# A deformable convolution prepared per batch, with the next layer's weight mixing beside its gathers

## The chip, the core and the metric

The kernel runs on one core of a Trainium2 chip. The core has a matrix engine (PE, with its own weight loads, PEld), a vector engine (DVE), a scalar engine (ACT), a general engine (POOL) and a queue that mainly starts transfers (SP); each works through its own queue of instructions in order, and they meet through semaphores. The metric is device time in microseconds (us) of one execution. The lower it is the better.

## The reference

A network of four layers on an input of 2 x 64 x 64 x 128 (two images, here called batches, of 4096 tokens with 128 channels), in float32. Layer 0 is a selective scan in four directions, layer 2 a state-space scan joined with a long spectral convolution, layer 3 attention and a mixture of experts. Layer 1, which the change rebuilds, is a deformable convolution on the group-normalised result x of layer 0, added to that result:

```python
offsets = conv(x, offset_w, 'SAME') + offset_b      # 3x3, 128 -> 18 channels
dy, dx = offsets[..., 0], offsets[..., 1]           # per pixel and tap
py, px = row + ky + dy, column + kx + dx
y0, x0 = floor(py), floor(px);  wy, wx = py - y0, px - x0
val = gather(y0, x0) * (1-wy)*(1-wx) + gather(y0, x0+1) * (1-wy)*wx
    + gather(y0+1, x0) * wy*(1-wx)   + gather(y0+1, x0+1) * wy*wx
out = einsum('bhwkc,kcf->bhwf', val, kernel) + bias # 9 taps, 128 -> 128
```

`gather` returns 0 outside of the image. Of layer 2 only one part matters here: before its convolution runs, 16 filters' matrices (`M_phi_plus`, `M_phi_minus`, four 128 x 128 each) are scaled and summed into mixed weights that depend on inputs alone.

## The kernel before

The activations X lie in SBUF as 64 tiles of 128 tokens x 128 channels (`k.X`, opened in pool `x01`), batch 0 in tiles 0 to 31, batch 1 in 32 to 63. `tile_hybrid_kernel` (L1375) calls `zero_table`, `layer0`, `layer1`, the function `work` inside `mixing_weights`, `norm_tokens` and then `layer2`.

**Who sets the order.** Outside of a few hand-ordered stretches (`tc.manual_schedule()`, in the scans of layers 0 and 2) a scheduler places the instructions when the kernel is built: each engine's queue is fixed then. Program order is the priority, and a later instruction that is ready may fill a gap. Tile pools are stacked in memory. A pool that is opened where a closed pool lay waits until all users of that pool are done. `bufs` is the number of copies of a tile that are used in turn.

**Layer 1** (L459) has a preparation and a gather loop.

The preparation runs over b = 0, 1:
- `to_channels` (L90; PE transposes L95, copies L72 alternating between DVE and ACT) makes `xt`, 128 channels x 4096 tokens.
- `zero_frame` clears the border of the padded image `xp` (66 x 66), on POOL. `groupnorm` (L126) takes statistics (L132, L133), runs a short chain on DVE, PE and ACT (L136 to L87) and scales `xt` in place (L146).
- POOL copies `xt` into `xp` (L485). PE transposes `xt` back to tokens, and copies make `xk`; eight transfers (L499, on SP's queue) write it into `table`, a tensor in DRAM of 2 x 67 x 67 cells with 4 x 128 numbers each: a cell holds the four neighbours that one bilinear sample needs. The table's border was zeroed at the start of the kernel by `zero_table`.
- The offset convolution: 8 column groups x 9 taps, matmuls of 128 x 18 weights on 512 columns (L505), output on 18 partitions; copies to `ot`; 32 transposes back to tokens (L510), and the offset bias (L511) gives `off`.

After both batches, DVE works out for all 64 tiles at once (tiles of 576 columns) the integer cell and the fractions (L526 to L537), the cell number `idx` (L538, L539) and the four weights `wt` (L543).

The gather loop runs over t = 0 to 63. Nine indirect transfers from POOL (L553) fetch 128 cells of 512 numbers each into `G` (3 buffers). DVE multiplies by the weights into `V` (L560, 2 buffers). PE sums the four neighbours and transposes in one step (L572, 36 matmuls against the identity), ACT copies to `vt` (L573), nine matmuls apply the kernel (L576), one adds the bias from a row of ones (L577), and DVE adds the result to X (L578). PSUM, of eight banks, is given out as 6 for the preparation, then 6 for `pv1` and 2 for `po2`.

**Mixing weights.** `mixing_weights` (L601) opens its pools `f2c` and `f2w` below those of layer 1. `work` is called after `layer1`, but its instructions can fill gaps earlier. It loads (L665, L666 for the 16 filters f), sums on DVE (L654, L656), scales (L669), adds and subtracts (L671, L672) and stores to DRAM. **`norm_tokens`** (L583) takes statistics of every tile of X (L590, L591) in a small pool `l2n` of its own, and from them the scale and shift for layer 2.

Of the kernel before, what the change touches and what calls it, by code (L numbers as in the profile page):

```python
# [158 lines left out]
def layer0(k):  # L159
# [3 lines left out]
    with ExitStack() as es:  # L163
# [26 lines left out]
        Y = big.tile([P, 2, L], F32, name="Y")  # L190
        zs = dr.tile([2, P, B * L], F32, name="zs")

        for b in range(B):
            Xb = X[:, b * NTB : (b + 1) * NTB, :]
            with ExitStack() as e2:
# [23 lines left out]
                for h in range(2):  # L219
# [6 lines left out]
                    for q in range(8):  # L226
# [10 lines left out]
                        nc.scalar.activation(U[:, h, q * N : (q + 1) * N], pc, AF.Silu, bias=k.v("conv_b")[:, h : h + 1])  # L237

# [167 lines left out]
            with ExitStack() as e2:  # L406
                wk = e2.enter_context(tc.tile_pool(name=f"l0f{b}", bufs=2))
                ps = e2.enter_context(tc.tile_pool(name=f"l0fs{b}", bufs=6, space=PSUM))
                for q in range(8):
# [24 lines left out]
                    nc.vector.tensor_tensor(o, po.rearrange("p (a c) -> p a c", c=C), o, ALU.add)  # L434

# [3 lines left out]
def zero_table(k, pool, table):  # L439


    nc = k.nc
    z = pool.tile([P, 4 * 4 * C], F32, name="zero")
    nc.gpsimd.memset(z, 0.0)
    flat = table.rearrange("a c -> (a c)")
    cell = 4 * C
    for b in range(B):
        at = b * TS * TS * cell

        for y in (0, TS - 2):  # L450
            rows = flat[at + y * TS * cell : at + (y + 2) * TS * cell].rearrange("(p f) -> p f", p=P)
            nc.gpsimd.dma_start(out=rows, in_=z[:, : 2 * TS * cell // P])

        edge = flat[at + (TS + TS - 2) * cell :]
        dst = bass.AP(edge.tensor, edge.offset, [[TS * cell, TS - 3], [1, 4 * cell]])
        nc.gpsimd.dma_start(out=dst, in_=z[: TS - 3, :])


def layer1(k, table):  # L459
    tc, nc, ins, X = k.tc, k.nc, k.ins, k.X  # L460
    with ExitStack() as es:
        enter = es.enter_context
        cst = enter(tc.tile_pool(name="l1c", bufs=1))
        wt = cst.tile([P, NT * 9, 4], F32, name="wt")
        idx = cst.tile([P, NT * 9], I32, name="idx")
        w_k = cst.tile([P, 9, C], F32, name="w_k")
        nc.sync.dma_start(out=w_k, in_=ins["kern1"].rearrange("t c f -> c t f"))

        with ExitStack() as e2:
            pre = e2.enter_context(tc.tile_pool(name="l1p", bufs=1))  # L470
            ps = e2.enter_context(tc.tile_pool(name="l1ps", bufs=6, space=PSUM))
            gmat = pre.tile([P, P], F32, name="gmat1")
            nc.sync.dma_start(out=gmat, in_=ins["gmat"])
            w_o = pre.tile([P, 9, 18], F32, name="w_o")
            nc.sync.dma_start(out=w_o, in_=ins["offw1"].rearrange("t c f -> c t f"))
            base = pre.tile([P, 2, NT, 9], F32, name="base")
            nc.sync.dma_start(out=base, in_=ins["base"])
            off = pre.tile([P, NT, 18], F32, name="off")
            for b in range(B):
                xt = pre.tile([P, L], F32, name="xt1")  # L480
                to_channels(k, ps, xt, lambda i: X[:, b * NTB + i, :], NTB)
                xp = pre.tile([P, 66, 66], F32, name="xp1", bufs=2)
                zero_frame(nc, xp)
                groupnorm(k, pre, ps, gmat, xt, "gn1")
                nc.gpsimd.tensor_copy(xp[:, 1:65, 1:65], xt.rearrange("p (h w) -> p h w", w=WW))  # L485

                xk = pre.tile([P, NTB, C], F32, name="xk")
                for g in range(0, NTB, 4):
                    pt = ps.tile([P, N], F32, name="pt1", tag="ps")
                    for j in range(4):  # L490
                        nc.tensor.transpose(pt[:, j * P : (j + 1) * P], xt[:, (g + j) * P : (g + j + 1) * P], k.ident)
                    k.copy(xk[:, g : g + 4, :].rearrange("p a c -> p (a c)"), pt)
                cells = table[b * TS * TS : (b + 1) * TS * TS, :].rearrange("(y x) c -> y x c", x=TS)
                for j in range(4):
                    dy, dx = divmod(j, 2)
                    for yy in range(2):
                        y0 = 2 - dy + yy
                        dst = cells[y0 : y0 + 63 : 2, 2 - dx : 66 - dx, j * C : (j + 1) * C]
                        nc.sync.dma_start(out=dst.rearrange("t x c -> x t c"), in_=xk[64 * yy : 64 * yy + 64, :, :])  # L499
                ot = pre.tile([18, L], F32, name="ot1")  # L500
                for q in range(8):
                    po = ps.tile([P, N], F32, name="po1", tag="ps")
                    for t in range(9):
                        ky, kx = divmod(t, 3)
                        nc.tensor.matmul(po[:18, :], w_o[:, t, :], xp[:, 8 * q + ky : 8 * q + ky + 8, kx : kx + WW], start=t == 0, stop=t == 8)  # L505
                    k.copy(ot[:, q * N : (q + 1) * N], po[:18, :])
                for g in range(0, NTB, 16):
                    pt = ps.tile([P, N], F32, name="pt2", tag="ps")
                    for j in range(16):
                        nc.tensor.transpose(pt[:, j * 18 : (j + 1) * 18], ot[:, (g + j) * P : (g + j + 1) * P], k.ident[:18, :18])  # L510
                    nc.vector.tensor_tensor(  # L511
                        off[:, b * NTB + g : b * NTB + g + 16, :],
                        pt[:, : 16 * 18].rearrange("p (a o) -> p a o", o=18),
                        k.r("offset_b").unsqueeze(1).to_broadcast([P, 16, 18]),
# [1011 lines left out]
```

## Time and profile before

| what | us |
|---|---|
| three runs | 15930.12, 15930.33, 15936.03 (median 15930.33) |
| the profiled execution | 15934.86 |
| its span in the profile | 15933.1 |
| PE busy | 12090.7 (76%) |
| DVE busy | 13888.6 (87%) |
| ACT busy | 9835.1 (62%) |
| POOL busy | 13460.0 (84%) |
| layer 0 (from the span's start) | to 4493.2 |
| layer 1, preparation | 4493.2 to 4693.60 |
| layer 1, gathers, first to last start | 4693.60 to 5663.64 |
| layer 1, last add to X (L578) | 5686.36 |
| first POOL work of layer 2 (L1101) | 5725.74 |

The span is the time from the first to the last recorded instruction; the execution is 1.8 us longer. Busy shares are means over stages with different limits: POOL's 84% comes mostly from the multiplications of the two scans, in layers 0 and 2, and says nothing of layer 1. A stage has to be read by itself, by its chain of waits (which work ended last, and what released it), its groups of instructions and its timeline. The mean granted PE clock over the span is 0.905 of full speed. The program has 190559 instructions.

### The profile page before, as it was taken

How to read it: one execution, taken by the hardware profiler on the slowest of the kernel's cores; microseconds unless marked ns; L12 is line 12 of the kernel's file. 1: busy time of each engine (PE TensorE's matmuls, PEld its weight loads, DVE VectorE, ACT ScalarE, POOL GpSimd, SP SyncE). 2: the span in 40 equal slices, each digit the busy share in tenths (PEclk: the TensorE clock that was granted, in tenths of full speed). 3: DMA queues.
4: the chain of work that ended last, by engine and by line, in shares of the span. 5: the costliest groups of instructions: out<-in, count | busy, mean ns of one | idle time of the engine just before them, and what ended most of it. 6: DMA issues, size and time to landing. Idle time of an engine off the chain costs nothing.

```text
span 15933.1 us, 190559 instructions
## 1 busy us (share of the span) xinstructions
PE 12090.7 (76%) x69566; PEld 7172.8 (45%) x69566; DVE 13888.6 (87%) x12159; ACT 9835.1 (62%) x15911; POOL 13460.0 (84%) x5142
## 2 busy tenths in 40 slices
PE   7666656666668854557887779879778898888897
PEld 2222222222238831334554546546445555555565
DVE  7999968999853379999999999999999999999974
ACT  5666526565500047777777677777777777777752
POOL 6888828888728889999999999999999999999960
PEclk9999989999988866778988889989999999999998
DMA  2111111111145544455565556556666665665543
GB/s 78 72 69 69 67 43 69 69 72 67 64 129 160 162 139 151 166 169 190 191 191 181 184 180 199 197 184 205 191 195 196 191 203 197 191 203 195 189 162 129
DMA packets 1211034, 2373.41 MB, mean 149 GB/s; under 512 B 346728, under 2 KB 923368, under 8 KB 1043952
## 3 DMA queue, kind: packets, MB, share of 16 engines
q1 hardware_dynamic: 1162672, 2206.74, 42.2%
q0 software_dynamic: 46560, 153.18, 3.3%
q8 instruction: 549, 8.99, 0.2%
q14 instruction: 389, 3.19, 0.1%
q10 hardware_dynamic: 864, 1.32, 0.0%
HBM read 2018.49 MB, written 342.41 MB: 148 GB/s over the span
## 4 chain that ended last, share of the span: by engine, by line
POOL 42%; DVE 16%; PE 14%; issue 6%; DMA 3%; ACT 3%; SPq 0%; POOLq 0%; DVEq 0%; ACTq 0%
POOL S L1101 36%; DVE S L1157 9%; PE pef L985 5%; DVE S L374 5%; POOL G L553 4%; DMA row<-drow 2%; PE Z L1119 2%; PE acc L958 2%; PE yp L403 1%; DVE M L388 1%; PE pw L784 1%; PE po L505 1%; POOL S L363 1%; POOL S L1107 1%; ACT ze L1125 0%
## 5 line engine op out<-in xcount | busy, mean ns | idle before, releaser
L1157 DVE TENSOR_TENSOR_SCAN S<-dA,S 128x512 f32<-128x512 f32 x8192 | 9222.6, 1198 | 391.9 <-ACT dA L1155 209.7
L1101 POOL TENSOR_TENSOR S<-row,g 128x4096 f32<-128x4096 f32 x1024 | 9102.4, 8896 | 255.6 <-DMA row<-drow 217.2
L1155 ACT ACTIVATE dA<-row,a_t 128x512 f32<-128x512 f32 x8192 | 5617.1, 692 | 2150.0 <-DVE S L1157 2113.9
L1119 PE MATMUL Z<-S,cv 128*32 128x256 f32 x32768 | 2498.8, 435 | 1488.5 <-ACT ze L1125 1248.9
L985 PE MATMUL pef<-hk,ur 128*128 128x256 f32 x14336 | 3508.6, 388 | 140.4 <-ACT e L965 122.0
L985 PEld LDWEIGHTS pef<-hk,ur 128*128 128x128 f32 x14336 | 2642.3, 191 | 1080.1 <-issue 564.8
L374 DVE TENSOR_TENSOR_SCAN S<-dA,S 128x1024 f32<-128x1024 f32 x1024 | 2339.2, 2284 | 243.5 <-ACT dA L372 98.1
L363 POOL TENSOR_TENSOR S<-du,br 128x1024 f32<-128x1024 f32 x1024 | 2407.8, 2354 | 138.2 <-DVE M L388 82.3
L1119 PEld LDWEIGHTS Z<-S,cv 128*32 128x32 f32 x32768 | 1000.9, 121 | 2690.9 <-issue 1290.0
L403 PE MATMUL yp<-M,ident 128*128 128x512 f32 x4096 | 2067.7, 629 | 2.9 <-DVE M L388 2.9
L403 PEld LDWEIGHTS yp<-M,ident 128*128 128x128 f32 x4096 | 821.8, 201 | 2087.8 <-issue 2049.1
L372 ACT ACTIVATE dA<-dt,an 128x511 f32<-128x511 f32 x2048 | 1406.9, 687 | 208.1 <-DVE S L374 131.2
L388 DVE TENSOR_TENSOR M<-S,pcn 128x1024 f32<-128x1024 f32 x1024 | 1250.6, 1221 | 106.4 <-DVE S L374 3.2
L332 PE MATMUL pcn<-cs,sel 80*128 80x512 bf16 x1024 | 408.5, 399 | 1174.6 <-DVE M L388 1157.6
L1125 ACT COPY ze<-Z 128x512 f32<-128x512 f32 x1024 | 1123.1, 1097 | 223.4 <-PE Z L1119 193.8
L958 PE MATMUL acc<-e,mw 128*128 128x512 f32 x1920 | 1039.3, 629 | 30.8 <-ACT e L965 30.2
L553 POOL DMA_INDIRECT G<-table,idx x576 | 795.9, 1382 | 261.1 <-issue 174.8
L985 PEld LDWEIGHTS pef<-hd,ur 128*128 128x128 f32 x4096 | 757.5, 194 | 493.0 <-issue 232.3
L985 PE MATMUL pef<-hd,ur 128*128 128x256 f32 (+1 forms) x4096 | 876.4, 340 | 102.6 <-ACT e L965 96.6
L560 DVE TENSOR_TENSOR V<-G,wt 128x4608 f32<-128x4608 f32 x64 | 317.5, 4960 | 602.5 <-DMA G<-table,idx 602.5
L376 ACT COPY stt<-S 128x2 f32<-128x2 f32 x896 | 168.9, 189 | 1081.5 <-DVE S L374 1078.5
L572 PE MATMUL pv<-ident,V 128*128 128x128 f32 x4608 | 612.6, 299 | 64.8 <-issue 59.7
(327 smaller groups left out, 8221.6 us busy)
## 6 DMA issues: line engine op xcount, KB each, us to landing
row<-drow SPq DMA_DIRECT2D x1024, 1024.0 KB
br<-bc SPq DMA_DIRECT2D x256, 1024.0 KB
zd<-ze SPq DMA_DIRECT2D x1024, 256.0 KB
hk<-in_phi_dram SPq DMA_DIRECT2D x128, 576.5 KB
hk<-in_phi_dram SPq DMA_DIRECT2D x96, 704.5 KB
hd<-in_phi_dram SPq DMA_DIRECT2D x512, 128.5 KB
mw<-wdr SPq DMA_DIRECT2D x480, 128.0 KB
hk<-in_phi_dram SPq DMA_DIRECT2D x160, 320.5 KB
```

Of the source, the lines that this page charges most:

```text
L363: nc.gpsimd.tensor_tensor(S, du, br[:, n % 4, :].unsqueeze(1).to_broadcast([P, 2, T]), ALU.mult)
L372: nc.scalar.activation(dA[:, h, rest], dt[:, h, rest], AF.Exp, scale=an[:, kk * 2 + h, n : n + 1])
L374: nc.vector.tensor_tensor_scan(flat, dflat, flat, 0.0, ALU.mult, ALU.add)
L388: nc.vector.tensor_tensor(M, S, pcn.unsqueeze(1).to_broadcast([P, 2, T]), ALU.mult)
L403: nc.tensor.matmul(yp[:, h, :], k.ident, M[:, h, :], start=False, stop=n == 15)
L553: nc.gpsimd.indirect_dma_start(out=G[:, o, :], out_offset=None, in_=table, in_offset=bass.IndirectOffsetOnAxis(ap=idx[:, t * 9 + o : t * 9 ...
L958: nc.tensor.matmul(acc.rearrange("p a s -> p (a s)"), ms[f][:, o, :], e, start=box["first"], stop="whole" in box and (f, o) == todo[-1])
L985: nc.tensor.matmul(pe[:, a, 256 - n :], ur[:, par, j, :], h[:, at : at + n], start=i == 0, stop=i + 1 == len(mm))
L1101: nc.gpsimd.tensor_tensor(S, row.unsqueeze(1).to_broadcast([P, 2, R, T]), g.unsqueeze(2).to_broadcast([P, 2, R, T]), ALU.mult)
L1119: nc.tensor.matmul(Z[32 * j : 32 * j + 32, q], cv[:, h, s], S[:, h, :, s], start=h == 0, stop=h == 1)
L1155: nc.scalar.activation(dA, row[:, j % R, :], AF.Exp, scale=a_t[:, h, d : d + 1])
L1157: nc.vector.tensor_tensor_scan(s, dA, s, 0.0, ALU.mult, ALU.add)
```

## The change

In words:
- Layer 0: tile Y moves from pool `l0b` to a pool of its own, opened per batch after the preparation of that batch's scan and closed at the end of the batch.
- There are two tables in DRAM, one per batch, and `zero_table` clears both.
- Layer 1's preparation runs per batch to the end: each batch has its own `off`, `cell`, `frac`, `rest`, `idx{b}`, `wt{b}`, half as wide. The pools of the gather loop are opened before the preparation, which gets a pool `l1p` above them, closed before the loop's code. The gathers of batch b name `table[b]` and `idx{b}`. PSUM is given out once: 3 banks for the preparation, 3 for `pv1`, 2 for `po2`.
- `base` is loaded per batch, before the loop; `xp` has one buffer in place of two.
- The kernel's bias is added to X on DVE, after `to_channels` has read it and before the group normalisation; the matmul with ones goes away.
- The copy into `xp` is on ACT, no longer on POOL.
- The offset convolution puts four column groups side by side in the PE array: weights padded with zeros from 18 to 32 columns, group j on output partitions 32j to 32j+31. Two rounds of 36 matmuls in place of eight of nine; each round has one copy, four full transposes and one add.
- In the gather loop G has 4 buffers and is multiplied in place; V is gone.
- `mix`, the former `work`, is called inside the loop at t = 36, and opens `f2c` and `f2w` there, above layer 1's remaining pools.

```diff
@@ layer0
-        Y = big.tile([P, 2, L], F32, name="Y")
...
+            yb = es.enter_context(ExitStack())
+            Y = yb.enter_context(tc.tile_pool(name=f"l0y{b}", bufs=1)).tile([P, 2, L], F32, name="Y")
...
+            yb.close()
@@ layer1
-def layer1(k, table):
+def layer1(k, table, mix):
...
         cst = enter(tc.tile_pool(name="l1c", bufs=1))
-        wt = cst.tile([P, NT * 9, 4], F32, name="wt")
-        idx = cst.tile([P, NT * 9], I32, name="idx")
+        gp = enter(tc.tile_pool(name="l1g", bufs=4))
+        wk = enter(tc.tile_pool(name="l1w", bufs=2))
+        ps = enter(tc.tile_pool(name="l1ps", bufs=3, space=PSUM))
+        gs = enter(tc.tile_pool(name="l1gs", bufs=3, space=PSUM))
+        po_ = enter(tc.tile_pool(name="l1go", bufs=2, space=PSUM))
+        over = enter(ExitStack())
+        pre = over.enter_context(tc.tile_pool(name="l1p", bufs=1))
...
+        w_o = cst.tile([P, 9, 32], F32, name="w_o")
+        nc.vector.memset(w_o, 0.0)
+        nc.sync.dma_start(out=w_o[:, :, :18], in_=ins["offw1"].rearrange("t c f -> c t f"))
...
+            bases.append(pre.tile([P, 2, NTB, 9], F32, name="base", bufs=2))
+            nc.sync.dma_start(out=bases[b], in_=ins["base"][:, :, b * NTB : (b + 1) * NTB, :])
+        for b in range(B):
+            Xb = X[:, b * NTB : (b + 1) * NTB, :]
+            xt = pre.tile([P, L], F32, name="xt1")
+            to_channels(k, ps, xt, lambda i: Xb[:, i, :], NTB)
+
+            nc.vector.tensor_tensor(Xb, Xb, k.r("bias1").unsqueeze(1).to_broadcast([P, NTB, C]), ALU.add)
+            xp = pre.tile([P, 66, 66], F32, name="xp1")
+            zero_frame(nc, xp)
+            groupnorm(k, pre, ps, gmat, xt, "gn1")
+            nc.scalar.copy(xp[:, 1:65, 1:65], xt.rearrange("p (h w) -> p h w", w=WW))
...
+            cells = table[b].rearrange("(y x) c -> y x c", x=TS)
...
-                for q in range(8):
-                    po = ps.tile([P, N], F32, name="po1", tag="ps")
-                    for t in range(9):
-                        ky, kx = divmod(t, 3)
-                        nc.tensor.matmul(po[:18, :], w_o[:, t, :], xp[:, 8 * q + ky : 8 * q + ky + 8, kx : kx + WW], start=t == 0, stop=t == 8)
-                    k.copy(ot[:, q * N : (q + 1) * N], po[:18, :])
+            for g in range(2):
+                po = ps.tile([P, N], F32, name="po1", tag="ps")
+                for t in range(9):
+                    ky, kx = divmod(t, 3)
                     for j in range(4):
+                        q = 4 * g + j
+                        nc.tensor.matmul(po[32 * j : 32 * j + 32, :], w_o[:, t, :], xp[:, 8 * q + ky : 8 * q + ky + 8, kx : kx + WW], start=t == 0, stop=t == 8)
+                ot = pre.tile([P, N], F32, name="ot1", bufs=2)
+                k.copy(ot, po)
+                pt = ps.tile([P, N], F32, name="pt2", tag="ps")
+                for i in range(4):
+                    nc.tensor.transpose(pt[:, i * P : (i + 1) * P], ot[:, i * P : (i + 1) * P], k.ident)
...
+            cell = pre.tile([P, 2, NTB, 9], F32, name="cell")
...
+            idx = cst.tile([P, NTB * 9], I32, name=f"idx{b}")
             nc.vector.tensor_copy(idx, tf.rearrange("p t o -> p (t o)"))
+            wt = cst.tile([P, NTB * 9, 4], F32, name=f"wt{b}")
...
+        over.close()
+        for t in range(NT):
+            b, i = divmod(t, NTB)
+            if t == NTB + 4 and mix is not None:
+                mix(es)
+            G = gp.tile([P, 9, 4 * C], F32, name="G")
...
+            V = G.rearrange("p o (q c) -> p (o q) c", c=C)
+            nc.vector.tensor_tensor(V, V, wts[b][:, i * 9 : (i + 1) * 9, :].rearrange("p o q -> p (o q)").unsqueeze(2).to_broadcast([P, 36, C]), ALU.mult)
...
-                nc.tensor.matmul(po, k.ones, k.r("bias1")[0:1, :], start=False, stop=True)
@@ mixing_weights
-    cst = es.enter_context(tc.tile_pool(name="f2c", bufs=1))
-    wp = es.enter_context(tc.tile_pool(name="f2w", bufs=2))
-
-    def work():
+    def work(es):
+        cst = es.enter_context(tc.tile_pool(name="f2c", bufs=1))
+        wp = es.enter_context(tc.tile_pool(name="f2w", bufs=2))
@@ tile_hybrid_kernel
-                    table = dr.tile([B * TS * TS, 4 * C], F32, name="table")
+                    table = [dr.tile([TS * TS, 4 * C], F32, name=f"table{b}") for b in range(B)]
...
-                with ExitStack() as e2:
-                    if two:
-                        mix = mixing_weights(k, dr, e2)
-                    if "1" in stages:
-                        layer1(k, table)
-                    if two:
-                        weights = mix()
+                if "1" in stages:
+                    layer1(k, table, mix)
```

## The prediction, made before the changed kernel was run

> **What bounds the kernel now.** The change touches layer 1, so I first cut the span by the chain of waits: layer 0 ends at 4493.2 us (last L434), layer 2's first work on POOL starts at 5725.7. Between them the chain reads (start, length, what):
>
> ```profile
> 4518.65 61.97 PE po L505 x144
> 4582.71 4.89 PE pt L95 x28
> ...
> 4609.20 61.97 PE po L505 x144
> ...
> 4693.60 6.46 POOL G L553
> ```
>
> The reader is to see a preparation of 200.4 us (4493.2 to 4693.60) in which the offset convolution is on the path once per batch, then 64 tiles of gathers. The last gather starts at 5663.64, so a tile takes (5663.64 - 4693.60 + 1.2)/64 = 15.2 us. The groups of the gather stage say which engine sets that (busy, mean ns | idle before, and on whom):
>
> ```profile
> L553 POOL DMA_INDIRECT G<-table,idx x576 | 795.9, 1382 | 261.1 <-issue 174.8 <-DVE smf L656 86.0 <-DMA G<-table,idx 0.3
> L572 PE MATMUL pv<-ident,V 128*128 128x128 f32 x4608 | 612.6, 299 | 64.8 <-issue 59.7
> L560 DVE TENSOR_TENSOR V<-G,wt 128x4608 f32<-128x4608 f32 x64 | 317.5, 4960 | 602.5 <-DMA G<-table,idx 602.5
> ```
>
> POOL waits for nobody after the first gather: 174.8 of its idle time is issue (0.30 before each of 576), 86.0 is before the first. DVE waits for gathers for 602.5 us, and PE is behind DVE. So POOL sets the pace. The timeline of both engines shows its 15.2 us:
>
> ```profile
> 4701.61 0.88 DVE L656 SCALAR_TENSOR_TENSOR smf<-m,w,smf 128x256 f32<-128x256 f32 x2
> 4701.63 0.95 POOL L553 DMA_INDIRECT G<-table,idx  x1 [0.30 <-issue]
> 4702.41 0.74 DVE L669 TENSOR_SCALAR smf<-smf,sg 128x1024 f32<-128x1024 f32 x1
> 4702.89 1.08 POOL L553 DMA_INDIRECT G<-table,idx  x1 [0.30 <-issue]
> ...
> 4713.08 4.96 DVE L560 TENSOR_TENSOR V<-G,wt 128x4608 f32<-128x4608 f32 x1 [9.93 <-DMA G<-table,idx]
> 4714.27 4.58 POOL L553 DMA_INDIRECT G<-table,idx  x1 [0.30 <-issue]
> 4719.16 0.95 POOL L553 DMA_INDIRECT G<-table,idx  x1 [0.30 <-issue]
> ```
>
> A gather costs 0.95 + 0.30 = 1.25, nine 11.25. The one that starts inside the multiply L560 ends only after it: 4714.27 + 4.58 = 4718.85, multiply's end 4718.04 plus 0.81. That adds 3.6 to 4.8 once per tile.
>
> **The change, part by part.**
>
> *Preparation of batch 0 (table, indices, column tiles, base, ACT copy).* Before, the one index array and the one table make the first gather wait for both batches. Afterwards it needs table 0 and indices 0. I rebuild its start from rows. Transposes of 32 tiles and their copies: the chain gives 4.9 us (L95) plus copies, 4493.9 to 4500.1. The bias add on DVE is new: 128x4096 against L560's 128x4608 in 4.96 us, so 4.96 x 4096/4608 = 4.4, to 4504.5. Remaining channel statistics (six L132, 3.65) to 4508.1. The small chain L133 to L87 took 4.4 us here with mixing work between its steps, but 3.8 in layer 0 without it (2264.57 to 2268.35); 3.8, to 4511.9. Scaling L146 2.4, to 4514.3. ACT now makes the padded copy, worked out at 3.6 us from its 128x512 (0.63) and 128x1024 (1.06) copies, before it helps with the token-major copies, whereas POOL did it in some 4 to 5 us; transposes and copies then take about 8 us, and the table's eight DMAs go out at about 4522. Before:
>
> ```profile
> 4520.48 35.11 SPq L499 DMA_DIRECT2D table<-xk  x8
> ```
>
> ```profile
> 4540.00:4550.00 10.00, 10.00 (x25) 2.25 (x24) 0.68 (x1) 0.25 (x1) 0.00 (x0) 1.00 0.99 216
> ```
>
> In that row of windows (span, busy of PE, PEld, DVE, ACT, POOL, clock, DMA share, GB/s) the DMA engines are full; they are from 4520 until about 4561, so the 8.4 MB (32 tiles x 64 KB x 4 corners) take 40.5 us whatever is computed beside them. With issue at 4522 the table is complete at 4562.5.
>
> The indices come sooner. Convolution: 144 passes of 430 ns = 61.97 us become 72 x 2 groups in four column tiles. Layer 3's last matmuls have this form already:
>
> ```profile
> 15862.60 1.90 PE L1325 MATMUL ph<-w,xw 128*32 128x512 f32 x10
> ```
>
> Ten of them in 1.90 us: four start within 0.02 us every 0.43. So 144/4 x 0.43 = 15.5 us (31 if only two run side by side); behind the token-major transposes on PE it ends at about 4537. Transposes and L511 take 4 us, then come the DVE steps up to the index: 0.45 to 0.75 each at 576 columns, half as wide about 6.6 us in all (up to 15 with batch 1's work between): 4548 to 4556. So the convolution, though it shrinks by 46 us, is no longer what ends last: the table write is. First gather about 4563.5 for 4693.60: **-130.1**. If the write is slower beside batch 1's work, some us come back; if the issue is 8 us earlier, the gain is 138. Preparation's ends: -120 to -140.
>
> *Gather loop (one G in place, four G, bias out).* The count of gathers and multiplies is the same: 0. The multiply still reads G and wt, both in SBUF, at the same shape. G is now freed by PE's L572 and no longer by DVE: hold per slot is 17.5 (gathers and landing) + 5 + 10.5 = 33 us; four slots come round in 60, so 27 us of slack cover it. The removed L577 counts -0.5, at the end only.
>
> *Batch 1's preparation beside gathers.* Some 35 us of PE (10 transposing, 15.5 convolution, the rest), against 2.2 us spare per tile x 32 = 70. DVE has 602 us of waiting. It costs only where a DVE operation holds a gather: L146 once (2.4), the cell arithmetic in halves. +3.3 (0 if all falls before the first gather, 15 if every locking operation lies over one).
>
> *Mixing weights, moved from 4493 to 4735 to beside batch 1's gathers.* Their SP loads and stores go behind the table's on SP's queue, which does nothing else then. Layer 2 needs the weights some 700 us later: cover is ample. They cost POOL stalls. Here **rule and trace** differ. The Trainium skill, "SBUF — State Buffer", section "Who interferes with whom", says that a DVE instruction with two SBUF inputs contends with a GpSimd instruction that reads SBUF, and that the shared pair is held for the whole instruction. That speaks against this move. The rows: L560 and L669 held a gather to their end, but two of L656, with two SBUF inputs, ran beside a gather of 0.95. By the rows, a pass f has L654 0.34, L669 0.74, L671 and L672 0.68 each, 2.44 us; an operation of length d that falls anywhere in a pitch of 1.25 costs d²/2.5 on average, 0.64 per f, x 16 = 10. Less 1.3 paid already for the four passes that lay beside gathers before: **+9**. By the rule three L656 of 0.48 join: 14 in all, +13. Ends: 0, and 16 x 2.44 = 39 (by the rule 62). I take +9.
>
> *A consequence that the diff doesn't spell out.* The pools are stacked. Before, f2c and f2w lay under layer 1, and the memory of norm_tokens' pool was that of f2c, free once mixing was done; its statistics ran between gathers:
>
> ```profile
> 4749.49 0.29 DVE L590 BATCH_NORM_STATS2 st<-X 128x6 f32<-128x128 f32 x1
> ...
> 15625.94 0.26 DVE L107 BATCH_NORM_STATS2 ln_st<-X 128x6 f32<-128x128 f32 x1
> ```
>
> Now layer 1's own l1c lies at the bottom, with w_k in it, which the last L576 reads. So norm_tokens can start only when layer 1 has ended. Its 64 statistics at layer 3's pitch of 0.26 (L107, 27 of them from 15625.2 to 15631.9) are 16.6 us, of which 1 lay at the end before: **+15.6** (0 if still interleaved; 35 if the aggregates between them, 0.18 busy each, cost a full 0.29 more).
>
> *Layer 0's Y in a pool of its own:* batch 1's weights now load 3 us later (after L432, 2254.0, not L428, 2250.9), needed from 2265: 0.
>
> Sum: -130.1 + 3.3 + 9 + 15.6 - 0.5 = -102.7. Profiled execution 15934.86 (span 15933.1 and 1.8 around it), so 15832. Its median is 4.5 lower (15930.33): **15828**.
>
> **Rivals.**
>
> *1. Batch 0's gathers still wait for batch 1's preparation*, because the queues are in order and the table's second write precedes. For: batch 1's DVE work is ready early. Against: POOL has nothing to do but these gathers. Batch 1's transposes and scaling (17) and its write (40.5) then lie in front, first gather about 4621: 15885. Chance 0.09.
>
> *2. DVE in bursts.* Mixing's operations back to back hold POOL for their whole length, or a DVE operation that waits for mixing's load holds the multiply behind it: before the first gather L656 and L654 did wait for m. Mixing then costs 39 to 62 in place of 9, batch 1's part some more: about 15870. Chance 0.13.
>
> *3. norm_tokens stays hidden:* 15828 - 15.6 = 15812. Against: the stacking above. Chance 0.09.
>
> *4. Slower: PE paces the tiles through G.* PE frees G and needs 12.8 us of work per tile at this clock:
>
> ```profile
> 5015.00:5177.00 162.00, 137.53 (x997) 131.54 (x997) 62.04 (x44) 14.49 (x33) 133.27 (x95) 0.85 0.55 157
> ```
>
> 137.53/162 x 15.1 = 12.8 at a granted clock of 0.85. It decides above 15.0 per tile, a clock under 0.73. It eats the whole gain when 64 tiles lose 103, at 16.6 per tile, clock 0.66; at 0.6 it is 18.1, +200, 16028. For: the convolution joins PE's work. Against: no window of the stage is under 0.80. Chance 0.05.
>
> **How the numbers follow.** The main case has 0.64, with its own range 15806 to 15870 (costs of the two moved parts from 0 to 54, preparation ±10). To hold 8 in 10, the low end takes in rival 3 and the high end rivals 1 and part of 2: 15788 to 15890. Within 0.2% (32 us, about what this measurement can tell) lies only a meeting of several losses, 0.03; slower 0.04, nearly all rival 4; faster 0.93.
>
> **What would show it.** First gather at 4563 ± 10 with the last table DMA just before it (a DVE releaser there means that indices gate); 64 tiles still 15.0 to 15.3 long; L505 in some 16 us per batch; gathers of 1.1 to 1.7 us beside L669, L671, L672; 64 L590 in a row after the last L578. It would be wrong if the multiply's start shifts: it comes 3.8 us after a tile's last gather starts, when the next tile's fourth gather is about to; if it met the third instead, each tile would wait some 1.1 us longer, 70 in all, a loss that nothing in the diff announces.

## The result, and the profile after

The changed kernel takes 15833.31 us (median of four runs, 15825.24 to 15840.11) against 15930.83 before (also of four, the three above and one more): the ratio is 0.9937 with a 95% interval of 0.9924 to 0.9949, 97.5 us less. The forecast was 15828. The profiled execution took 15825.24 us, span 15823.2. One run of e7 below, of 16495.21 us, fell in a slower state with a granted clock of 0.754 where its other three had 0.907 to 0.909, and is left out.

The groups of layer 1 in the changed kernel (busy, mean ns | idle before, and on whom), in the order of those shown of before, with the convolution last (L569 is the gather, L583 PE's sums, L576 the multiply):

```profile
L569 POOL DMA_INDIRECT G<-table,idx x576 | 805.5, 1399 | 203.1 <-issue 170.6 <-DVE xt L146 27.5 <-DVE wf L682 0.9
L583 PE MATMUL pv<-ident,G 128*128 128x128 f32 x4608 | 566.1, 281 | 62.3 <-issue 61.6
L576 DVE TENSOR_TENSOR G<-G,wt 128x4608 f32<-128x4608 f32 x64 | 317.4, 4960 | 572.9 <-DMA G<-table,idx 499.6 <-issue 73.3
...
L519 PE MATMUL po<-xp,w_o 128*32 128x512 f32 x288 | 42.0, 627 | 4.5 <-issue 3.9
```

Once it has started, POOL still waits for nobody, and it is busy 9.6 us longer: 805.5 for 795.9. A gather that nothing disturbs is busy for about 0.946 us; where it is busy longer it is called held below, for the time above 0.946. All that was won lies ahead of the first gather. The timeline of that preparation:

```profile
4499.88 4.42 DVE L492 TENSOR_TENSOR X<-X,rv 128x4096 f32<-128x4096 f32 x1
...
4511.95 2.41 DVE L146 TENSOR_SCALAR xt<-xt,gn_mg,gn_rs 128x4096 f32<-128x4096 f32 x1
...
4520.11 7.93 PE L519 MATMUL po<-xp,w_o 128*32 128x512 f32 x72
...
4520.83 35.97 SPq L510 DMA_DIRECT2D table<-xk  x8
...
4554.76 0.31 DVE L553 CAST idx<-tf 128x288 int32<-128x288 f32 x1
...
4565.57 1.07 POOL L569 DMA_INDIRECT G<-table,idx  x1 [27.49 <-DVE xt L146]
```

Seventy-two matmuls take 7.93 us, so a batch's convolution takes 15.9 us and not 61.97. The index is there at 4555.1, ten microseconds before the first gather. The profile names L146 of batch 1 as the releaser, which ended at 4564.74, but the table's transfers end there too. In the windows (the last two columns are DMA share and GB/s):

```profile
4562.00:4563.00 1.00, 0.00 (x0) 0.00 (x0) 0.93 (x3) 0.00 (x0) 0.00 (x0) 0.50 0.64 173
4563.00:4564.00 1.00, 0.00 (x0) 0.00 (x0) 1.00 (x1) 0.00 (x0) 0.00 (x0) 0.50 0.44 131
4564.00:4565.00 1.00, 0.20 (x1) 0.20 (x2) 0.74 (x1) 0.15 (x1) 0.00 (x0) 0.50 0.01 4
```

The last packet of the write ends at 4564.18, 43 us after its issue. This trace alone can't tell which of the two the gather waited for; the experiments' traces can. In all nine of them whose first gather comes after the write (all but e2 and e11), and here, it starts 1.39 or 1.40 us after the last packet, while L146 ends from 0.74 to 1.68 us ahead of it (in e4, where the first gather comes 53.9 us after L146, the packet is that of batch 1's write). In e7, for instance, L146 is done at 4562.84, the last packet ends at 4563.13, and the first gather starts at 4564.52:

```profile
4560.43 2.41 DVE L146 TENSOR_SCALAR xt<-xt,gn_mg,gn_rs 128x4096 f32<-128x4096 f32 x1
...
4564.52 1.07 POOL L569 DMA_INDIRECT G<-table,idx  x1 [28.35 <-issue]
```

So the table's write is what the first gather waits for.

The other end of layer 1, on DVE:

```profile
5569.33 0.29 DVE L588 TENSOR_TENSOR X<-po,X 128x128 f32<-128x128 f32 x1 [9.78 <-PE po L587]
5569.54 0.47 DVE L600 BATCH_NORM_STATS2 st<-X 128x6 f32<-128x128 f32 x2
5569.93 0.16 DVE L601 BATCH_NORM_AGGREGATE mv<-st 128x2 f32<-128x6 f32 x1
5570.02 0.26 DVE L600 BATCH_NORM_STATS2 st<-X 128x6 f32<-128x128 f32 x1
```

After the last add the 64 statistics follow in a row, as forecast, until 5586.2. The shift for layer 2 and layer 2's first work on POOL come behind them:

```profile
5588.44 0.23 DVE sh L603
...
5622.89 8.83 POOL S L1110
```

The stages, from both profiles (us):

| stretch | before | after | difference |
|---|---|---|---|
| start to first gather | 4693.60 | 4565.57 | -128.0 |
| first to last gather | 970.04 | 980.25 | +10.2 |
| last gather to end of last add | 23.0 | 23.8 | +0.8 |
| last add to first POOL work of layer 2 | 39.1 | 53.3 | +14.2 |
| layers 2 and 3 | 10207.3 | 10200.3 | -7.0 |

The first four add up to -102.8. The last row is not the change: in the experiments below, where layers 2 and 3 do the same work, the stretch lies between 10196 and 10211 (all but e3). That is also why totals of a single pair of runs are good to some 10 us only, and stages are read from profiles.

### The profile page after: what moved, and what is told of

Same layout as the page of the kernel before. It is cut to its first block, busy times and chain, and to the rows that moved or that the text cites. A ratio compares the mean times of both kernels' runs of the same rounds, so it can differ in the third digit from the quotient of the medians.

```text
span 15823.2 us, 190331 instructions
## 1 busy us (share of the span) xinstructions
PE 11939.5 (75%) x69390; PEld 7104.0 (45%) x69390; DVE 13880.2 (88%) x12178; ACT 9839.5 (62%) x15907; POOL 13460.9 (85%) x5140
## 4 chain that ended last, share of the span: by engine, by line
POOL 35%; PE 12%; DVE 11%; DMA 3%; ACT 2%; issue 2%; SPq 0%; POOLq 0%; ACTq 0%; DVEq 0%
POOL S L1110 34%; DVE S L1166 10%; PE pef L994 6%; PE Z L1128 2%; DMA row<-drow 2%; PE acc L967 2%; PE pw L793 1%; POOL S L1116 1%; ACT ze L1134 1%; ACT dA L1164 1%; DMA w<-in_w_b_dram 0%; PE acc L1029 0%; ACT e L974 0%; DMA e<-mdr 0%; PE pt L95 0%
## 5 line engine op out<-in xcount | busy, mean ns | idle before, releaser
L569 POOL DMA_INDIRECT G<-table,idx x576 | 805.5, 1399 | 203.1 <-issue 170.6
L576 DVE TENSOR_TENSOR G<-G,wt 128x4608 f32<-128x4608 f32 x64 | 317.4, 4960 | 572.9 <-DMA G<-table,idx 499.6
L974 ACT COPY e<-pef 128x512 f32<-128x512 f32 x960 | 557.8, 587 | 109.9 <-PE pef L994 61.5
## 6 DMA issues: line engine op xcount, KB each, us to landing
mw<-wdr SPq DMA_DIRECT2D x480, 128.0 KB
```

## The experiments

Each is the changed kernel with one edit, but for two combinations (e8, e9) and one edit of the kernel before (e11). Totals are medians of four or more runs, in e7 of three. "Stage" is the time from the first gather's start to the last one's. In the changed kernel it is 980.25 us; in e1, e4, e5 and e10, which change neither a gather nor the length of a multiply, it is 983.8 to 986.4, so a difference of up to 6 us between stages says little.

**e1: the pool of norm_tokens below layer 1.**

```diff
-    with tc.tile_pool(name="l2n", bufs=1) as pre:
...
+def norm_tokens(k, rs, sh, pre):
...
+                with tc.tile_pool(name="l2n", bufs=1) as l2n:
...
+                        layer1(k, table, mix)
...
+                        norm_tokens(k, rs, sh, l2n)
```

> The changed kernel with one edit: the pool of norm_tokens is opened below layer 1's pools, so its memory is nobody else's. In the changed kernel 64 statistics run in a row after the last add to X, and the shift for layer 2 ends 19.3 us after that add; before it was 3.3 us. Theory (the memory under layer 1 holds them back): the statistics lie between the gathers again, the shift follows the last add in 3 to 4 us, layer 2's first POOL work 15 to 16 us earlier, total about 15817. Rival (the scheduler puts them last because layer 1's code precedes them, whatever the memory): still 64 in a row, total unchanged at about 15833. The gather stage stays at 980 us in both.

15817.82 us (ratio to before 0.9929, 0.9912 to 0.9946), 15.5 less than the changed kernel. The end of layer 1 on DVE:

```profile
5574.28 0.29 DVE L588 TENSOR_TENSOR X<-po,X 128x128 f32<-128x128 f32 x1 [9.21 <-PE po L587]
5574.60 0.29 DVE L599 BATCH_NORM_STATS2 st<-X 128x6 f32<-128x128 f32 x1
5574.93 0.18 DVE L600 BATCH_NORM_AGGREGATE mv<-st 128x2 f32<-128x6 f32 x1
```

One statistic remains after the last add. The theory holds: the memory of the pool kept them back, not the place of the code. In the profile the stretch from the last add to layer 2's first POOL work is 39.3 us, 14.0 shorter; layer 2 starts 9 us earlier and not 15, since the gather stage is 986.4 us here, 6.1 longer. That the medians differ by 15.5, as forecast, is in part chance.

**e2: the convolution without column tiles.**

```diff
-            for g in range(2):
+            for g in range(8):
...
-                        nc.tensor.matmul(po[32 * j : 32 * j + 32, :], w_o[:, t, :], xp[:, 8 * q + ky : 8 * q + ky + 8, kx : kx + WW], start=t == 0, stop=t == 8)
+                    nc.tensor.matmul(po[:32, :], w_o[:, t, :], xp[:, 8 * g + ky : 8 * g + ky + 8, kx : kx + WW], start=t == 0, stop=t == 8)
...
```

> The changed kernel with the offset convolution one column group at a time (8 groups of 9 matmuls, output on 32 partitions), the rest as it is. Changed kernel: convolution 15.9 us, index at 4555.1, table written at about 4561.5, first gather at 4565.6. Theory (the convolution is off the path only because it shrank; the split by batch alone would leave it as the gate): convolution about 62 us, index at about 4601, first gather about 4602, 36 us later, total about 15869. Rival (the table write gates anyway and the column tiles bring nothing): first gather within 5 us of 4565.6.

15932.42 us (1.0001, 0.9992 to 1.0009): all of the gain is gone. The first gather came at 4607.3, right behind the index (4607.0) and 42 us later than in the changed kernel, somewhat more than the theory's 36. The other 59 are in the gather stage, 1039.2 us long. The groups from 4490 to 4800 and PE's timeline:

```profile
L517 PE MATMUL po<-xp,w_o 128*32 128x512 f32 x288 | 129.8, 605 | 0.0
L567 POOL DMA_INDIRECT G<-table,idx x80 | 107.4, 1343 | 101.5 <-PE pv L581 61.4 <-issue 21.9 <-DVE idx L551 16.3
```

```profile
4685.06 1.16 PE L581 MATMUL pv<-ident,G 128*128 128x128 f32 x8
4686.14 0.43 PE L522 MATMUL pt<-ident,ot 32*128 32x32 f32 x4
4686.51 7.91 PE L517 MATMUL po<-xp,w_o 128*32 128x512 f32 x18
4694.35 0.71 PE L581 MATMUL pv<-ident,G 128*128 128x128 f32 x4
```

Batch 1's convolution takes PE for 7.91 us at a time, and the sums L581 get a few matmuls in between. PE is what frees G, so POOL waits 61.4 us for it, in two pauses of 28 and 33 us ahead of tiles 4 and 5. My expectation looked at the first gather alone.

**e3: the loads and stores of the mixing without its arithmetic** (layer 2 then runs on other weights).

> The changed kernel without the arithmetic of the 16 mixed matrices: what was loaded is stored as it is, so the loads and stores stay and the five kinds of DVE operation go (the outputs of layer 2 are not the reference's). Changed kernel: first to last gather 980.2 us, of which 12 us are gathers held beside these operations. Theory (DVE's operations hold gathers, the two-input sums too): 968 us, total 12 lower, about 15821. Rival 1 (the transfers of the mixing slow the gathers): 980 as now. Rival 2, the reading of the prediction's rows (the two-input sum with a scalar does not hold a gather): also about 968, but in the changed kernel's own trace gathers beside that sum alone would be at 0.95 us.

The gather stage is 970.5 us, 9.7 less than the changed kernel's 980.2. POOL's busy time falls by as much, from 805.5 to 795.7:

```profile
L569 POOL DMA_INDIRECT G<-table,idx x576 | 795.7, 1381 | 203.2 <-issue 173.3 <-DVE xt L146 27.4 <-DMA G<-table,idx 1.2
```

Outside of the multiplies gathers are held for less than 1 us in all. So it is the arithmetic, not the transfers. The total, 15806.52 (0.9921, 0.9905 to 0.9938), is 27 lower: 11 lie ahead of layer 2, the rest in layers 2 and 3 (10186.5 us), on other data. What in these other data does it stays open.

**e4: one table again.**

```diff
-                    table = [dr.tile([TS * TS, 4 * C], F32, name=f"table{b}") for b in range(B)]
+                    whole = dr.tile([B * TS * TS, 4 * C], F32, name="table")
+                    table = [whole[b * TS * TS : (b + 1) * TS * TS, :] for b in range(B)]
...
-                    in_=table[b],
+                    in_=whole,
...
```

> The changed kernel with one table for both batches again (indices offset by batch, everything else per batch): batch 0's gathers then also wait for batch 1's table write. This is the prediction's rival 1 made on purpose. Theory: first gather when batch 1's write is done, that is 4565.6 plus batch 1's transposes and copies (8) and write (41 to 50), about 4617 to 4622, total about 15885; the gathers of batch 0 no longer run beside the second write, and the 8 us and more that a multiply then waits for its gathers are gone. Rival (the split of the table brings little, since the indices of both batches are what counted): first gather below 4590.

15885.08 us (0.9969, 0.9957 to 0.9982); the first gather came at 4616.3, when batch 1's write had ended (the last two columns of the windows are DMA share and GB/s):

```profile
4614.00:4615.00 1.00, 0.00 (x0) 0.00 (x0) 0.00 (x0) 0.00 (x0) 0.00 (x0) 0.50 0.21 61
4615.00:4616.00 1.00, 0.00 (x0) 0.00 (x0) 0.38 (x4) 0.46 (x2) 0.00 (x0) 0.50 0.00 0
```

```profile
4616.31 1.07 POOL L569 DMA_INDIRECT G<-table,idx  x1 [80.56 <-DVE y L633]
```

Batch 1's index had been there since 4597.2, so it was not what the gather waited for. The theory holds; that the total meets it to a tenth of a microsecond is chance, since the six runs lie between 15871 and 15898. One part of it does not: multiplies still wait for their gathers for up to 8.2 us, now beside the loads of the mixing. The split of the table is worth 52 us given that all else is per batch.

**e5: the multiply in the other two-input form.**

```diff
-            nc.vector.tensor_tensor(V, V, wts[b][:, i * 9 : (i + 1) * 9, :].rearrange("p o q -> p (o q)").unsqueeze(2).to_broadcast([P, 36, C]), ALU.mult)
+            wv = wts[b][:, i * 9 : (i + 1) * 9, :].rearrange("p o q -> p (o q)").unsqueeze(2).to_broadcast([P, 36, C])
+            nc.vector.scalar_tensor_tensor(V, V, 1.0, wv, ALU.mult, ALU.mult)
```

> The changed kernel with the multiply of each tile written as a two-input operation with a scalar (scalar_tensor_tensor: G times 1.0 times wt, same shapes, in place). The prediction read from two rows of before that this form does not hold a gather. By that reading: no gather is held for 3.6 to 4.8 us once per tile, a tile takes what PE needs (12.8 us) and not 15.2, the gather stage falls from 980 to about 820 to 840 us, total about 15690. By the rule of the Trainium skill that it was weighed against (SBUF, who interferes with whom: any DVE instruction with two SBUF inputs holds the shared pair for its whole length): the gather that starts inside is held to its end plus 0.81 us as now, stage within 10 us of 980, total about 15833 (if the form is as fast, 4.96 us).

15834.86 us (0.9938, 0.9921 to 0.9954), stage 984.4: no difference.

```profile
4867.25 4.96 DVE L577 SCALAR_TENSOR_TENSOR G<-G,wt 128x4608 f32<-128x4608 f32 x1 [8.67 <-DMA G<-table,idx]
4867.65 5.38 POOL L569 DMA_INDIRECT G<-table,idx  x1 [0.30 <-issue]
4872.13 0.28 DVE L589 TENSOR_TENSOR X<-po,X 128x128 f32<-128x128 f32 x1
```

The gather that starts 0.40 us into the operation ends 0.82 us after it, just as beside the plain product. As the rule would have it, this form holds a gather too, and the prediction's reading of its rows falls.

**e6: nine short multiplies.**

```diff
-            nc.vector.tensor_tensor(V, V, wts[b][:, i * 9 : (i + 1) * 9, :].rearrange("p o q -> p (o q)").unsqueeze(2).to_broadcast([P, 36, C]), ALU.mult)
+            wv = wts[b][:, i * 9 : (i + 1) * 9, :].rearrange("p o q -> p (o q)")
+            for o in range(9):
+                nc.vector.tensor_tensor(V[:, 4 * o : 4 * o + 4, :], V[:, 4 * o : 4 * o + 4, :], wv[:, 4 * o : 4 * o + 4].unsqueeze(2).to_broadcast([P, 4, C]), ALU.mult)
```

> The changed kernel with the multiply of each tile cut into nine of 128x512, one per gather, each of which can start when its gather has landed. The same DVE work with nine fixed costs, about 9 x 0.68 = 6.1 us for 4.96. Theory (a gather is held only by a DVE operation that runs at the moment it asks, some 0.1 us after its start, and then to that operation's end): a landing comes 3.8 us after a gather's start, 0.05 to 0.3 us after the start of the gather three later, which has then been granted; few gathers are held, a tile takes PE's 12.8 us, stage about 820 to 850 us, total about 15690. Rival (what counts is the sum of DVE time, however it is cut): each of nine holds a gather for about 0.5 us, 4.5 us per tile, stage 980 to 1010.

15662.25 us (0.9833, 0.9816 to 0.9849): 171 less than the changed kernel and the fastest of all. The stage is 809.6 us. DVE does more work than in the changed kernel, nine operations of 693 ns for each of 4960, but the gathers are held for 89.4 us altogether and not 260.6:

```profile
L569 POOL DMA_INDIRECT G<-table,idx x576 | 634.3, 1101 | 203.9 <-issue 168.8 <-DVE xt L146 27.6 <-DMA G<-table,idx 3.4
```

Not few of them are held, as the theory had it, but 344 of 576 (by over 0.05 us), each for little. The timeline shows why:

```profile
5026.26 1.13 POOL L569 DMA_INDIRECT G<-table,idx  x1 [0.30 <-issue]
5027.69 1.28 POOL L569 DMA_INDIRECT G<-table,idx  x1 [0.31 <-issue]
5029.27 0.95 POOL L569 DMA_INDIRECT G<-table,idx  x1 [0.30 <-issue]
```

A short operation can hold a gather only for what is left of it: 0.18 and 0.33 us here. POOL still sets the pace: 576 x 1.25 us plus 89.4 is 809.4. A tile takes 12.7 us, a little less than the 12.8 of PE that I had expected as the limit. That figure belonged to a granted clock of 0.85; here PE is busy for 419.11 of 487 us, at a higher clock. The same window of the gather stage, before, changed and here (the third and second columns from the end are clock and DMA share):

```profile
4853.00:5340.00 487.00, 407.56 (x2950) 390.32 (x2951) 182.04 (x131) 43.67 (x98) 399.29 (x289) 0.86 0.56 160
```

```profile
4853.00:5340.00 487.00, 384.56 (x2881) 368.89 (x2880) 167.96 (x66) 43.55 (x95) 398.95 (x290) 0.89 0.56 162
```

```profile
4853.00:5340.00 487.00, 419.11 (x3504) 413.13 (x3503) 248.45 (x390) 56.02 (x117) 380.33 (x351) 0.96 0.69 195
```

The granted clock is 0.96 in place of 0.86 and 0.89, with more matmuls in the window.

**e7: four of nine gathers multiplied on ACT.**

```diff
...
+            for j in range(16):
+                nc.scalar.activation(V[:, j, :], V[:, j, :], AF.Copy, scale=wv[:, j : j + 1])
+            nc.vector.tensor_tensor(V[:, 16:, :], V[:, 16:, :], wv[:, 16:].unsqueeze(2).to_broadcast([P, 20, C]), ALU.mult)
```

> The changed kernel with the first four gathers' blocks of every tile (16 of 36 blocks of 128x128) multiplied on ACT, one activation with a scale per block at about 0.45 us (7.2 us, with the copies 8.6 per tile), and the other 20 in one DVE multiply of 128x2560, about 2.8 us. Theory (the held gather waits for DVE's end): it is held about 1.7 us and not 3.9, a tile takes 13.0 us, close to what PE needs, stage about 840 to 850 us, total about 15700. Rival (ACT's copies of the transposed tile now queue behind its multiplies and PE's results wait): a tile takes 14 us or more, stage 900 or longer.

15720.40 us (0.9864, 0.9844 to 0.9884), stage 856.4, gathers held for 137.0:

```profile
L569 POOL DMA_INDIRECT G<-table,idx x576 | 681.9, 1184 | 203.8 <-issue 195.3 <-PE pv L586 4.6 <-ACT vt L587 0.6
```

Less DVE in one piece, less hold; the stage is a little longer than expected, and e6 is faster.

**e8: e6 and e1 together.**

> The nine short multiplies and the pool of norm_tokens below layer 1, together. The two act in different stages (between gathers, and after the last), so the sum: 15662 less the 15.5 that the pool gave alone, about 15647, with no 64 statistics in a row at the end. Rival: between the gathers the 128 small statistics operations now hold gathers or delay multiplies, and half or more of the 15 comes back: 15655 or more.

15748.58 us (0.989, 0.9874 to 0.9907). It is 86 slower than e6 alone. The theory is wrong, and the rival, which this total does not contradict ("15655 or more"), had reckoned with a loss of half of 15 us or more, not with 86. Gathers are held less than in e6 (73.9 us), but POOL stands still for another 112, always ahead of a tile's first gather:

```profile
5032.16 0.95 POOL L569 DMA_INDIRECT G<-table,idx  x1 [2.62 <-PE pv L585]
```

This is tile 32. PE has just ended the sums of tile 28, whose buffer it takes, while the multiplies are at tile 31. PE runs three tiles behind, and 51 of the 64 tiles wait for a buffer, mostly 1.2 to 3 us, once 25 (tile 4, beside batch 1's preparation). The sums of tile 30 take 12.0 us here, with pauses in them, and 8.2 in one piece in e6; with the matmuls of the convolution's kernel that makes the pace of 13.9 us per tile there. The profile names the landing of a gather ahead of some of these pauses and nothing ahead of most. What PE waits for, and how the statistics between the gathers bring it about, stays open.

**e9: e8 with the bias added later in the program.**

> The same with the bias added to X only after the batch's weights are worked out, no longer ahead of the statistics. The changed kernel's bias add stands in DVE's queue for 4.42 us ahead of six of the statistics. Theory (it is on the path of batch 0's table): scaling, table issue, table landing and first gather all 4.4 us earlier, first gather about 4559 to 4561; batch 1's add then lies beside gathers and holds one for up to 4 us. Net 0 to -4 against the kernel without this edit. Rival (the indices become the gate, or batch 1's scaling falls over the first gather): first gather not before 4563.

15755.04 us (0.9891, 0.9875 to 0.9908): nothing won over e8. The add was moved behind the weights in the code, yet it now runs behind the statistics and still ahead of L133, which closes them:

```profile
4506.69 4.41 DVE L559 TENSOR_TENSOR X<-X,rv 128x4096 f32<-128x4096 f32 x1
4511.01 0.37 DVE L133 BATCH_NORM_AGGREGATE gn_mv<-gn_st 128x2 f32<-128x48 f32 x1
```

The scaling L146 follows layer 0's last add by 18.8 us, in the changed kernel by 18.9. So the edit didn't take the 4.4 us off the path, and what that would bring stays untested.

**e10: three buffers of G.**

> The changed kernel with three buffers of G in place of four. The prediction costed the in-place multiply at nothing because PE frees a buffer 33 us after its first gather and four come round in 60. With three, a buffer comes round in 45 us. Theory (33 us hold, 12 us of slack): nothing lost in most tiles; in the first 20 tiles, where a multiply waits up to 6 us longer beside batch 1's table write, and PE also works on batch 1, a few gathers wait: stage 980 to 995, total 15833 to 15848. Rival (PE runs more than one tile behind, the hold is really 45 us or more): POOL waits for PE in most tiles, stage over 1010, total over 15860.

15828.48 us (0.9938, 0.9921 to 0.9954), stage 986.2; POOL waited for PE for 2.4 us in the whole stage:

```profile
L569 POOL DMA_INDIRECT G<-table,idx x576 | 810.0, 1406 | 204.8 <-issue 170.4 <-DVE xt L146 27.6 <-PE pv L583 2.4
```

The slack that the prediction worked out was there, even for one buffer less.

**e11: the kernel before, with nine short multiplies.**

> The kernel before, with only its multiply cut into nine, one per gather (V is still a tile of its own). Cut in the changed kernel this took the gather stage from 980 to 810. Theory (the held gather is a matter of how long DVE's operations are, and was there before the change as well): stage from 970 to 800 to 830, total about 15780. Rival (it took the changed kernel's four buffers or its PE order to make use of it): stage above 880.

16032.33 us (1.0062, 1.0045 to 1.0079): slower than before. The holds are nearly gone, some 14 us in all, but POOL stands still for about 338 more. The groups from 4700 to 5700:

```profile
L553 POOL DMA_INDIRECT G<-table,idx x537 | 519.6, 968 | 479.8 <-DVE st L591 300.9 <-issue 155.9 <-DVE V L561 20.6
L561 DVE TENSOR_TENSOR V<-G,wt 128x512 f32<-128x512 f32 x517 | 324.1, 687 | 519.0 <-PE pv L573 296.3 <-remote 211.9 <-DMA G<-table,idx 9.9
```

The multiply waits for PE to free V (296.3 us), and the gather for DVE to free G. Two short chains of buffers with DVE's fixed order between them pace the loop. The rival holds: the cut that wins 171 us in the changed kernel loses 102 here. Which of the changed kernel's differences it takes, the fourth buffer, the multiply in place or the order of the engines, wasn't tested apart.

## Why the prediction was right, and where it wasn't

The sum held because its large terms did, and because its smaller errors have both signs: the preparation won 2.1 us less than forecast, the gather stage lost 2.1 us less (10.2 for 3.3 + 9), and the end of the layer came to 15.0 for 15.6 - 0.5. That -102.8 meets the forecast's -102.7 is luck, all the more as some of the terms inside the gather stage were wrong.

- **Preparation:** -130.1 forecast, -128.0 measured. The steps: bias add 4.4 (4.42 measured), table issue 4522 (4520.8), convolution 15.5 (15.9), index 4548 to 4556 (4555.1). The write took 43.3 us, not 40.5, and that is where the 2.1 us come from: it is 2.8 us longer, and its earlier issue gives back 1.2. That the table and not the index ends last is as forecast (4564.18 and 4555.1, and the gather follows the table); without the tiles the index is last (e2). The table's part of the gain is confirmed by e4, the tiles' part by e2. The two don't add up, since each needs the other. The index per batch, the padded copy on ACT and the new division of PSUM were not tested apart.
- **The column tiles** were costed as a step of batch 0 that falls behind the table write. They are worth 99 us (e2), of which 42 are the first gather's. The part that the prediction passed over is batch 1: its "35 us of PE" against "2.2 us spare per tile" holds only with tiles. Without them PE holds G. This is the mechanism of rival 4, brought about by work and not by the clock.
- **Gather loop:** 0 forecast. The multiplies held gathers for 248.4 us after 245.6. That PE's release of the buffer costs nothing is confirmed by e10, which takes one buffer away; the multiply in place was not tested by itself. One term was missed: the first gather of before lasted 6.46 us, held by mixing work, and now lasts 1.07, worth -5.4.
- **Batch 1's preparation beside gathers:** +3.3 forecast, 0.6 of holds in the trace and a pause of 0.5. Beside the second table write and the mixing loads behind it, multiplies started up to 9.8 us after a tile's last gather had started, for 4 us usually. Buffers covered it. The -0.5 for the removed L577 is not seen: last gather to last add takes 0.8 us longer.
- **Mixing weights:** +9 forecast: 10 for the holds to come, less 1.3 for those that the mixing had cost before. The trace has 11.3 of holds; e3 gives 9.7 for the whole stage, good to some 6. So the 10 is about right and its reason half wrong. The 1.3 was too small: with the first gather it was 5.8, which is the term missed above. **The step that failed** is "two of L656, with two SBUF inputs, ran beside a gather of 0.95", taken as proof that this form does not hold one. In the changed kernel it does:

```profile
4716.71 1.67 DVE L666 SCALAR_TENSOR_TENSOR smf<-m,w,smf 128x256 f32<-128x256 f32 x4
4717.26 1.94 POOL L569 DMA_INDIRECT G<-table,idx  x1 [0.30 <-issue]
```

  The four end at 4718.38, the gather 0.82 later. In the rows of before the first L656 began 0.03 us ahead of the gather's start and the second 0.38 after it, so neither had been running for long when the gather came. What the prediction had left out is who comes first. The Trainium skill, "SBUF — State Buffer", section "Who interferes with whom", says, of DVE's two-port modes, that whoever issues first has the pair for the whole instruction and the other blocks. The traces bear out one half of this: a gather that comes second is held. The other half does not show in them, since a gather that came first did not lengthen a DVE operation:

```profile
5020.46 0.94 POOL L569 DMA_INDIRECT G<-table,idx  x1 [0.30 <-issue]
5020.64 4.96 DVE L576 TENSOR_TENSOR G<-G,wt 128x4608 f32<-128x4608 f32 x1 [9.85 <-DMA G<-table,idx]
5021.71 4.71 POOL L569 DMA_INDIRECT G<-table,idx  x1 [0.30 <-issue]
```

  Of the 64 multiplies 51 began like this one inside a gather, and took 4.94 to 4.96 us, no longer than the others. By its reading of the rows the prediction had holds of 10, by the rule 14; the 11.3 of the trace lie between.
- **norm_tokens:** +15.6 forecast; the shift is ready 19.1 us after the last add where it was 2.9, so 16.1; 14.2 reach layer 2. e1 confirms cause and size (-14.0 in this stretch).
- **Rivals:** 1 (batch 0 waits for batch 1) did not happen; it was priced at 15885, and e4, which brings it about, measured 15885.08. Rival 3 (the statistics stay hidden) did not happen either; it was priced at 15812, and e1, which brings it about, measured 15817.82. Rival 2 did not happen: DVE's bursts of mixing lie where the gathers are, but the longest hold by them was 2.5 us. Rival 4 did not happen in the changed kernel, where the clock of the stage rose (0.86 to 0.89 in the window shown under e6).

## What to carry to other kernels

When two batches are prepared and then used, ask of each shared object (a table, an index array) who waits for the whole of it; then ask who frees the buffers once the second preparation runs beside the first use, because an engine with room to spare on the mean can still hold them in bursts. A long DVE operation beside gathers can be worth cutting into pieces of the length of a gather: here that won more than the whole change. It did so only where the pieces don't wait for a buffer behind another engine (e11), so look at those waits first. A small pool's place in memory can decide when its work runs: look at what lay there before.

## What the runs showed of the hardware

- What decides is who came first. Over before, the changed kernel and e5, of the gathers that met a DVE operation which had been running for over 0.05 us and went on for 0.2 us or more, 240 of 243 were held, 218 of them to its end plus 0.81 or 0.82 us. The three that weren't met operations that read PSUM (L72, L525). Where none had been running just ahead, and one began within 0.05 us of the gather's start, 2 of 24 were held; where it began later, 1 of 156. Two of these three are the first gather of the kernel, busy for 1.07 us in nearly every run. The product, the sum with a scalar and the scaling all held gathers.
- Operations without a gap between them can go on holding: eleven in a row held the first gather of before for 5.5 us. They don't always: in the changed kernel a gather that starts at 4766.39 in a run of L666 is held for 0.34 us only, to the end of one operation, while the run goes on. What makes the difference stays open.
- The granted clock in the window 4853 to 5340 was 0.86 before, 0.89 after the change and 0.96 in e6. PE's pauses there (of over 0.05 us) number 39, 100 and 37, with 79, 102 and 68 us in all, so neither their number nor their sum orders the clock; what sets it stays open.
